# Filling the steps of a software pipeline: pieces cut to one step each, due at fixed steps or drawn by an account of TensorE time

## The chip, the core and the metric

The kernel runs on one core of a Trainium2 chip. The metric is the device time in microseconds of one execution. Three runs before the change took 5651.95, 5647.72 and 5645.32 us; the median is 5647.72 us. The profile is of one further execution.

The engines by the names of the profile: PE (TensorE, matrix products and transposes, with PEld for its weight loads), DVE (VectorE), ACT (ScalarE), POOL (GpSimd) and SP (SyncE, which issues nearly all transfers here). Each works through its own instructions in order and waits on semaphores for the others.

## What is computed

Four layers of attention follow each other on a state `x` of 2048 rows and 256 columns. All attend to the same 1601 context rows of 512 columns, and each adds its result to `x`. Layers 0, 2 and 3 have 16 heads of 64 and a column bias for a few token positions:

```python
q = hidden_states @ Wq;  k = encoder_hidden_states @ Wk;  v = encoder_hidden_states @ Wv
logits = einsum('bhqd,bhkd->bhqk', q, k) * HEAD_DIM ** (-0.5) + col_bias
probs = softmax(logits, axis=-1)
out = einsum('bhqk,bhkd->bhqd', probs, v) @ Wo + bo + residual
```

Layer 1 first divides each row of `x` by its root mean square. It has 16 query heads of 16 columns that share 4 heads of keys and values, and no bias. All is float32; in layer 1 the scores are formed from bfloat16 parts.

## The kernel before

**Units and steps.** A block is a pair of heads in layers 0, 2 and 3 (`Masked`, 8 blocks a layer) or one group of four query heads in layer 1 (`Grouped`, 4 blocks). A unit is one block on 512 of the 2048 queries, in `Grouped` one half of the block's heads on them: 4 units a block in `Masked`, 8 in `Grouped`, 32 a layer and 128 in all, numbered u0 to u127 here (layer 1 is u32 to u63). The 1601 keys are cut into 13 chunks, 12 of 128 and one of 65, and a unit passes through 13 steps, ca 0 to ca 12, one chunk a step. The loop at L1067 writes out 1664 such steps and a drain.

**What a step holds.** Three stages of neighbouring units overlap. In a step the loop emits the scores of a chunk of unit `ka`, the exponentials of a chunk of the unit before (15 steps later than its scores), and the product with the values (16 steps later). In a masked step this is on PE L751 (scores) and L869 (values); on ACT the copy of the scores to SBUF (L763) and the exponential (L841); on DVE the subtraction of the row maximum (L834) and the running maximum over chunks (L768); on POOL the running sum of the exponentials over chunks (L844 for chunks 0 and 1 together, then L846). A masked chunk is a tile `p` of 128 x 1024 in a pool of 17. At ca 0 and ca 1 PE also transposes the previous unit's maxima (L805) and spreads them (L818). In a grouped step PE does L784, L850, L855 and L869, DVE one reduction (L789) and ACT one exponential (L859). An instruction is held to the order written here on PE, ACT and DVE.

**Pieces.** What is left is cut into pieces, which the loop sprinkles over the steps, after the step's own work:

- for the next unit, `unit_groups`: load the transposed `x` (L735) and project the queries (L420 in masked units; L626, a split into parts, and stacks L529, L532, L645 in grouped ones);
- for a unit just finished, `finish_groups`: `denominators` (eight transposes of the sums, L888, reduced on DVE, L889, inverted, L890, and widened by POOL, L899), `divide` (four transposes, L907, and a product on DVE, L911) and two of `project` (L917, added to `xs` by DVE, L923);
- after the last block of a layer also `keep` or `normalize` (squares, `rms` with L679, and four `divide` of L689 and L691 for layer 1) or `rows_out`;
- for the next block, `key_groups`: the keys by 512 columns, one PE matmul of 512 columns a piece (L369, L559), and the values by two chunks (L384, L592), with their loads of the context (`context_slice`, L204).

PSUM holds two tiles `s`, one `b`, one `po` and one `pm`. All pieces work in the single `pm`, but for the transposes of the sums, which take one of the two `s` tiles that the scores use. A piece that wants `pm` waits until the engine that empties it, ACT or DVE, has done so.

**The order of the pieces.** `Pieces` (L970) keeps the queues `urgent`, `fill` and `later` and a credit. Unit pieces and finishing pieces enter `urgent` at ca 2; the next block's keys stand in `fill`, its values in `later` until ca 4 of the block's second unit. In every step but ca 0 and ca 1 after a masked unit, at least one piece is taken, `urgent` first, and more if what is left for the block is more than the steps. A key group of four pieces goes on over several steps.

## Time and profile before

| | us |
|---|---|
| median of three runs | 5647.72 |
| the profiled execution | 5653.54 |
| its span, first to last instruction | 5651.8 |
| from the start to the first step | 77.0 |
| u5 to u27 (steady masked units, layer 0) | 1003.8 |
| u28 to u35 (into layer 1) | 414.7 |
| u36 to u56 (steady grouped units) | 784.6 |
| u57 to u67 (out of layer 1) | 473.4 |
| u68 to u123 (steady masked units, layers 2 and 3) | 2459.1 |

A unit's time is the distance between the first score matmul of its first step and that of the next unit in the timeline of PE. A line of a group or of a timeline gives the source line, the engine, the operation, the tiles as out<-in, shapes, a count and the busy time; in square brackets or at the end stand the idle time before it and what ended that. In the view of waits a line names who waited for whom, with the total, the number and the longest wait in us. Matmul records overlap, so PE's work is better read from one start to the next than from durations.

### The profile page before, as it was taken

Reading aid. Unit: us, or ns where it says so; the run is one execution under the profiler, and the core shown is the slowest. Engines: PE = TensorE matmul, PEld = TensorE weight load, DVE = VectorE, ACT = ScalarE, POOL = GpSimd, SP = SyncE. Lnnn points to the kernel's source line nnn. Section 1 sums busy time; section 2 is a strip of 40 time slices with the busy share of each in tenths; the row PEclk is TensorE's granted clock in tenths of the full one; section 3 lists DMA queues with packets and bytes.
Section 4 is the critical chain, followed back from the end, with each engine's and each line's share of the span. In section 5 each row is a group of like instructions: output and inputs, shape, how many; then the busy total and the mean of one; then the engine's idle time right before and its main releaser. Section 6 shows DMA issues by size and latency. Waiting matters only on the chain.

```text
span 5651.8 us, 59516 instructions
## 1 busy us (share of the span) xinstructions
PE 5321.4 (94%) x22444; PEld 1865.2 (33%) x22444; DVE 4013.6 (71%) x4140; ACT 3196.2 (57%) x3513; POOL 2837.7 (50%) x1380
## 2 busy tenths in 40 slices
PE   6999999998889999999999999999999999999997
PEld 3333333332323333233233333333333333333332
DVE  3777777777765555555567777777777777777786
ACT  2666666665433434333456666666666666666665
POOL 1766666665410000000056666666666666666676
PEclk8999999999889999999999999999999999999998
DMA  4112211111100000001012111212111121111100
GB/s 135 32 57 60 59 49 53 55 56 44 39 20 5 9 9 9 9 13 52 15 51 61 56 54 49 57 56 59 46 56 55 54 59 49 53 56 52 54 17 15
DMA packets 209744, 252.88 MB, mean 45 GB/s; under 512 B 43529, under 2 KB 155401, under 8 KB 209456
## 3 DMA queue, kind: packets, MB, share of 16 engines
q1 hardware_dynamic: 206192, 243.69, 14.8%
q8 instruction: 177, 2.90, 0.2%
q0 software_dynamic: 1152, 3.28, 0.2%
q10 hardware_dynamic: 2112, 2.10, 0.1%
q14 instruction: 111, 0.91, 0.1%
HBM read 235.27 MB, written 13.76 MB: 44 GB/s over the span
## 4 chain that ended last, share of the span: by engine, by line
PE 78%; ACT 7%; POOL 7%; DVE 5%; issue 2%; DMA 0%; SPq 0%; ACTq 0%; POOLq 0%; DVEq 0%
PE po L869 24%; PE s L751 20%; PE pm L384 6%; PE pm L369 5%; PE pm L917 5%; POOL sums L844 4%; ACT p L763 4%; ACT p L841 3%; POOL sums L846 3%; PE s L850 2%; PE s L784 2%; PE pm L420 2%; PE s L805 2%; PE b L818 2%; PE s L855 2%
## 5 line engine op out<-in xcount | busy, mean ns | idle before, releaser
L846 POOL TENSOR_TENSOR sums<-sums,p 128x1024 f32<-128x1024 f32 (+1 forms) x1056 | 2499.2, 2367 | 1097.9 <-ACT p L841 1084.8
L763 ACT COPY p<-s 128x1024 f32<-128x1024 f32 (+1 forms) x1248 | 1263.4, 1012 | 1434.0 <-PE s L751 1138.3
L869 PE MATMUL po<-p,v 128*64 128x512 f32 (+1 forms) x6656 | 1821.7, 626 | 36.5 <-ACT p L841 34.7
L768 DVE TENSOR_TENSOR top<-s,top 128x1024 f32<-128x1024 f32 (+1 forms) x1056 | 1291.5, 1223 | 753.9 <-ACT p L763 749.4
L751 PE MATMUL s<-q,kT 64*128 64x512 f32 (+1 forms) x4992 | 1426.3, 648 | 117.6 <-DVE top L768 116.4
L834 DVE TENSOR_TENSOR p<-p,b 128x1024 f32<-128x1024 f32 (+1 forms) x1248 | 1504.7, 1206 | 2.4 <-PE b L818 2.0
L841 ACT ACTIVATE p<-p 128x1024 f32<-128x1024 f32 (+1 forms) x1248 | 1321.5, 1059 | 110.3 <-DVE p L834 109.4
L869 PEld LDWEIGHTS po<-p,v 128*64 128x64 f32 (+1 forms) x6656 | 332.0, 136 | 1032.1 <-issue 698.9
L899 POOL COPY by<-rden 128x512 f32<-128x512 f32 x128 | 78.5, 613 | 1111.8 <-DVE rden L897 1083.9
L751 PEld LDWEIGHTS s<-q,kT 64*128 64x128 f32 (+1 forms) x4992 | 370.7, 182 | 732.7 <-issue 454.6
L859 ACT ACTIVATE p<-s 128x1024 f32<-128x1024 f32 (+1 forms) x283 | 289.8, 1024 | 451.0 <-PE s L855 450.9
L844 POOL TENSOR_TENSOR sums<-p 128x1024 f32<-128x1024 f32 x96 | 226.5, 2360 | 434.2 <-ACT p L841 434.2
L789 DVE TENSOR_REDUCE row_top<-s 128x2 f32<-128x1024 f32 x261 | 318.6, 1221 | 122.9 <-PE s L784 121.9
L384 PEld LDWEIGHTS pm<-wv,ct 128*128 128x128 f32 (+1 forms) x2392 | 284.7, 187 | 218.9 <-issue 215.9
L384 PE MATMUL pm<-wv,ct 128*128 128x128 f32 (+1 forms) x2392 | 337.6, 286 | 0.5 <-ACT v L389 0.5
L369 PE MATMUL pm<-ct,wk 128*128 128x512 f32 (+1 forms) x736 | 315.8, 544 | 2.7 <-ACT kT L374 2.7
L917 PE MATMUL pm<-o,wo 128*128 128x512 f32 x512 | 292.0, 653 | 7.1 <-DVE xs L923 2.9
L859 ACT ACTIVATE p<-b 128x1024 f32<-128x1024 f32 (+1 forms) x133 | 136.2, 1024 | 217.8 <-PE b L855 217.8
L923 DVE TENSOR_TENSOR xs<-pm,xs 128x512 f32<-128x512 f32 x232 | 158.4, 683 | 90.4 <-PE pm L917 90.4
L806 DVE TENSOR_REDUCE ntop<-s 128x8 f32<-128x1024 f32 x96 | 117.6, 1225 | 130.9 <-PE s L805 130.6
L789 DVE TENSOR_REDUCE row_top<-b 128x2 f32<-128x1024 f32 x123 | 150.2, 1221 | 62.2 <-PE b L784 61.6
L420 PE MATMUL pm<-xT,wq 128*128 128x512 f32 x336 | 188.5, 644 | 0.0
(191 smaller groups left out, 3279.2 us busy)
## 6 DMA issues: line engine op xcount, KB each, us to landing
ct<-ctxT SPq DMA_DIRECT2D x288, 512.0 KB, 3.8
xT<-xT SPq DMA_DIRECT2D x104, 512.0 KB, 3.5
ct<-ctxT SPq DMA_DIRECT2D x48, 130.0 KB, 2.6
wk<-in_L_xattn_Wk_dram SPq DMA_DIRECT2D x24, 256.0 KB, 4.4
wv<-in_L_xattn_Wv_dram SPq DMA_DIRECT2D x24, 256.0 KB, 3.1
xT<-xs SPq DMA_DIRECT2D x12, 512.0 KB, 2.6
wq<-in_L_xattn_Wq_dram SPq DMA_DIRECT2D x24, 128.0 KB, 2.1
wo<-in_L_xattn_Wo_dram SPq DMA_DIRECT2D x24, 128.0 KB, 2.1
```

The costliest lines, as they stand in the source:

```text
L369: nc.tensor.matmul(u.pk[:, :n], u.wk[:, k, :], ct(k, a, n), start=(k == 0), stop=(k == NCT - 1),)
L384: nc.tensor.matmul(u.pv[:m, c - c0, :], ct(k, a, m), u.wv[:, k, :], start=(k == 0), stop=(k == NCT - 1),)
L751: nc.tensor.matmul(s[:m, h, :], self.u.kT[r, a : a + m], self.q[r, :], start=True, stop=(a != TAIL),)
L763: nc.scalar.copy(p[:m], s[:m])
L768: nc.vector.tensor_tensor(self.top[:m], s[:m], self.top[:m], ALU.max)
L789: nc.vector.tensor_reduce(self.top[:, :, q, k : k + 1], s, AX.X, ALU.max)
L834: nc.vector.tensor_tensor(self.p[c][:m], self.p[c][:m], self.less[:m], ALU.add)
L841: nc.scalar.activation(p[:m], p[:m], AF.Exp)
L844: nc.gpsimd.tensor_tensor(self.sums, self.p[0], p, ALU.add)
L846: nc.gpsimd.tensor_tensor(self.sums[:m], self.sums[:m], p[:m], ALU.add)
L869: nc.tensor.matmul(self.po[r, :], u.v[:m, c, r], self.p[c][:m, h, :], start=(c == 0), stop=(c == NT - 1),)
L917: nc.tensor.matmul(py, wo[:, ts(k, P)], self.o, start=True, stop=True)
```

## The change

- `Piece` is a function with a cost in units of about one key chunk. Every piece now starts and empties its PSUM tile itself. Keys are projected chunk by chunk (four matmuls of 128 columns, one copy), values chunk by chunk, queries in two halves of 256 columns. Before the first step, too, keys and values go chunk by chunk.
- `Pieces.at` puts a piece at a step of its own. Counted by ca of the unit in which they are emitted: the sums of the two heads at ca 3 and ca 4 (`denominators(0)`, `denominators(1)`), the query halves at ca 7 and 8, `divide` at ca 8, the projections at ca 10 and 11, the grouped stacks at ca 10, 11 and 12, normalisation from ca 12 on.
- The rest comes from `fill` when an account allows. In each step `share` is added (what is left, plus 7.0 a masked or 4.6 a grouped unit, over the steps left in the block), the cost of what is due is taken off, and a fill piece is taken while the credit is at least half its cost. The account is held between -1.5 and 1.5. `later` is released when the last unit of the previous block is finished.
- The denominators' transposes take `pm`, four at a time. The reciprocals no longer go through POOL, PE and DVE: SP writes them to DRAM, loads them back spread over the partitions, and POOL multiplies `oT` in place.
- The sums begin with a copy of chunk 0 on POOL, and chunk 1 is added as the others.
- The weights `wk` and `wv` have one buffer instead of two; a context tile holds two chunks; the loads of a block are issued three ahead, and `load_wo` at the block's third unit.

```diff
+Piece = namedtuple("Piece", "run cost")
...
-            u.wk = weights.tile([P, NCT, P], FP, name="wk")
-            u.wv = weights.tile([P, NCT, P], FP, name="wv")
+            u.wk = weights.tile([P, NCT, P], FP, name="wk", bufs=1)
+            u.wv = weights.tile([P, NCT, P], FP, name="wv", bufs=1)
...
+            def keys(c, ct):
...
+                pk = ps_m.tile([P, QB], FP, name="pm")[:, :m]
+                for k in range(NCT):
                     nc.tensor.matmul(
+                        pk, u.wk[:, k, :], ct(k)[:, :m], start=(k == 0), stop=(k == NCT - 1)
                     )
+                nc.scalar.copy(u.kT[:, a : a + m], pk)
...
+            return [(7 + j, Piece(lambda j=j: queries(j), 1.0)) for j in range(2)]
...
+            return found + [
+                (10, Piece(lambda: stacked(0), 0.5)), (11, Piece(lambda: stacked(1), 0.5)),
+                (12, Piece(last, 0.25)),
+            ]
...
+        return [
+            (10, Piece(squares, 0.0)), (11, Piece(rms, 2.0)),
+            *((12 + q, Piece(lambda q=q: divide(q), 0.0)) for q in range(QT)),
+        ]
...
+    def on_all_partitions(cols, to):
+        rows = dram.tile([2, P, QT], FP, name="cols", bufs=4)
+        with nc.allow_non_contiguous_dma(reason="1024 values, four at a time"):
+            nc.sync.dma_start(out=rows.rearrange("h p q -> p h q"), in_=cols)
+        for tile_, heads_ in to:
+            src = rows[heads_].rearrange("(o h) p q -> o (h p q)", o=1)
+            nc.sync.dma_start(out=tile_, in_=src.to_broadcast(tile_.shape))
...
-                if c == 1:
+                if c == 0:
                     self.sums = work.tile([P, 2, QB], FP, name="sums")
-                    nc.gpsimd.tensor_tensor(self.sums, self.p[0], p, ALU.add)
-                elif c:
+                    nc.gpsimd.tensor_copy(self.sums, p)
+                else:
                     nc.gpsimd.tensor_tensor(self.sums[:m], self.sums[:m], p[:m], ALU.add)
...
-        def denominators(self):
+        def denominators(self, h):
...
-                pt = ps_s.tile([P, 2, QT, P], FP, name="s")
...
+                pt = ps_m.tile([P, QT, P], FP, name="pm")
+                for q in range(QT):
+                    nc.tensor.transpose(pt[:, q, :], self.sums[:, h, ts(q, P)], ident)
+                nc.vector.tensor_reduce(rden[:, h, :], pt, AX.X, ALU.add)
+                if h == 0:
+                    return
                 nc.vector.reciprocal(rden, rden)
...
-            nc.gpsimd.tensor_copy(
-                self.by,
-                rden.rearrange("p h (q o) -> p q h o", o=1).to_broadcast((P, QT, 2, 64)),
-            )
+            by = work.tile([P, P, QT], FP, name="by", bufs=1)
+            on_all_partitions(
+                rden,
+                [(by[self.rows(h)].rearrange("r p q -> r (p q)"), slice(h, h + 1)) for h in range(2)],
+            )
+            self.by = by.rearrange("r p q -> r q p")
         def divide(self):
-            pr = ps_m.tile([P, QB], FP, name="pm")
...
-            nc.vector.tensor_tensor(self.o, pr, self.oT, ALU.mult)
+            oT = self.oT.rearrange("r (q p) -> r q p", p=P)
+            nc.gpsimd.tensor_tensor(oT, oT, self.by, ALU.mult)
...
+            found = [(1 + h, Piece(lambda h=h: self.denominators(h), 0.5)) for h in range(2)]
+            if not self.masked:
+                found = [(1, Piece(lambda: self.denominators(0), 1.0))]
+            found.append((6, Piece(self.divide, 0.0)))
+            return found + [(8 + k, Piece(lambda k=k: self.project(k), 1.0)) for k in range(NC)]
...
+        def step(self, step, share, cost):
+
+            self.credit = max(min(self.credit + share - cost, 1.5), -1.5)
+            for piece in self.due.pop(step, ()):
+                piece.run()
+                self.credit -= piece.cost
+            while self.fill and self.credit >= self.fill[0].cost / 2:
+                piece = self.fill.popleft()
+                piece.run()
+                self.credit -= piece.cost
...
+        if scoring and ca == 5 and ka + 1 < len(units):
             ahead = unit_of(ka + 1)
+            pieces.at(step - ca, ahead.layer.query_pieces(ahead))
         if valuing and cv == NT - 1:
+            pieces.at(step, valuing.finish() + after(kv))
+
+            if units[kv + 1 : kv + 2] and units[kv + 1][0] != units[kv][0]:
+                pieces.release()
+        share = 0.0
+        if scoring:
+            units_left = NB * len(scoring.layer.SUBS) - place - ca / NT
+            own = 7.0 if scoring.masked else 4.6
+            share = (pieces.left() + own * units_left) / (NT * units_left)
+        pieces.step(step, share, 1.0 if top and top.masked else 0.0)
```

## The prediction

> **What bounds the kernel now.** I read the page's busy shares first, then the waits, then PE's timeline step by step.

> ```profile
> PE 5321.4 (94%) x22444; PEld 1865.2 (33%) x22444; DVE 4013.6 (71%) x4140; ACT 3196.2 (57%) x3513; POOL 2837.7 (50%) x1380
> ```

> PE is the bound, and nearly everywhere. So only PE work, and waits that end on PE, move the time. These are the waits that the change aims at:

> ```profile
> ACT p L763 <- POOL sums L844: 174.5, 93, 2.5
> PE s L751 <- DVE top L768: 116.4, 71, 2.7
> PE pm L907 <- POOL by L899: 55.9, 79, 4.4
> ```

> One chain: at ca 3 POOL adds chunks 0 and 1 together and so frees chunk 0's tile too late for the score copy of ca 4. The copy is late, the maximum after it too, and L888 holds the other `s` tile. The scores of ca 5 wait 1.71. The next rows, from the timeline, show what the change brings instead: two pieces of one step that both want `pm`, with DVE to empty it.

> ```profile
> 2942.62 1.13 PE L751 MATMUL s<-q,kT 64*128 64x512 f32 x4
> 2944.69 1.12 PE L917 MATMUL pm<-o,wo 128*128 128x512 f32 x2
> 2945.38 1.22 DVE L768 TENSOR_TENSOR top<-s,top 128x1024 f32<-128x1024 f32 x1
> 2946.51 0.68 DVE L923 TENSOR_TENSOR xs<-pm,xs 128x512 f32<-128x512 f32 x1
> 2947.24 1.12 PE L917 MATMUL pm<-o,wo 128*128 128x512 f32 x2 [1.43 <-DVE xs L923]
> 2948.30 1.13 PE L751 MATMUL s<-q,kT 64*128 64x512 f32 x4
> ```

> DVE empties `pm` only after this step's running maximum, which waits for the score copy. `pm` is free 4.62 after the step's start; the step takes 5.68, where one piece gives 3.12.

> **Steady masked blocks (u5 to u27, u68 to u123, about 20 blocks).** Prices are starts to starts in u18: scores 1.06, values 1.01, so 2.07 a step; L805 or L818 1.02; a value chunk 1.09; a query matmul or projection 1.05; eight transposes 0.97, L907's four 0.59. A key chunk has the value chunk's form, eight instructions of 128 columns, so 1.09, against 1.06 for the old 512-column piece. The tail chunk is taken at 0.65, the bias at 0.15 a unit.

> Before, a unit has 13 x 2.07 + 2.04 + 0.15 + 2 x 1.05 + 0.97 + 0.59 + 2 x 1.05 = 34.9, a block four of these plus 12 x 1.06 + 0.65 + 13 x 1.09 = 27.5, so 167.0. Measured are (1050.5 for u4 to u27 + 2459.1) / 20 = 175.5: waits are 8.5 a block. After, the denominators are two times four transposes (2 x 0.59) and L907 is gone: 34.5 a unit; the fill is 25 x 1.09 + 0.65 = 27.9; together 165.9.

> Then I carried the account through by hand. A block repeats: units with 7, 6, 7 and 6 fill pieces. A fill piece falls into ca 3 or ca 4 beside a denominator five times a block (ca 3; ca 4; ca 3 and ca 4; ca 4), beside a projection at ca 10 once, and two keys share ca 12 once. Beside a denominator: PE is ready at 2.07 + 0.59 = 2.66; DVE's maximum of the step ends at 3.5 (scores 1.06, copy from 1.23, maximum from 2.28, in the steps about 2914), the reduction of 512 columns is 0.70 (as L791's of 520), so `pm` is free at about 4.25. In the rows above it is 4.62 (DVE was late there by a `divide` that is gone), in u29, projection then L559, 4.35. The wait is 1.6 (0.8 if the reduction ran ahead of the maximum, 2.0 by 4.62). Beside the projection it is 1.1 (u29 shows 1.16), between two keys, emptied by ACT, 0.45. A block: 5 x 1.6 + 1.1 + 0.45 = 9.6. Steps with less than one piece cost 0.4, where DVE's 1.21 + 1.22 outlast PE's 2.07. Half-clock windows are left at 0.5. So 165.9 + 10.5 = 176.4, +0.9 a block, **+18 in all**. The waits shown go, all 8.5 of them but the clock; `pm` is late next, for 9.6. Ends: -80 with 0.8, +55 with 2.0.

> What lies beside: POOL's copy of chunk 0 is 1.2 (twice L899's 0.61) and the multiply 1.2 (half of L846's 2.37), in 41 to 44 a unit where POOL has 28 to 31; chunk 0's tile is then free by 4.6 of ca 2 and asked for at ca 4. ACT gains about 0.6 a unit for shorter copies, with 28 of 43 busy. DVE loses L911's 0.69 and gains little.

> **The way over DRAM.** SP's queue gets a write of 256 pieces of 16 bytes, which waits for the reciprocal, then two loads, which wait for the write; behind them stand the next unit's `x` (ca 5) and the context loads. The reciprocal is done at 4.3 of ca 4. The nearest rows are the token indices (1 KB, 3.2 to land) and `wo` (16 KB, 1.7). Multiply at ca 8, 12 later: hidden. The `x` load is issued after about 4.3 + 0.4 + 2.4 + 0.9 = 8.0 and lands 3.5 later, at 11.5; the first query half wants it at ca 7, 11.05 after ca 4's start where ca 4 holds no fill (one unit a block), later elsewhere. 0.45 x 20 gives 9, halved for masked layers' first blocks and luck: **+5**, between 0 and, with 3.2 to land, 25. Context loads run three tiles, six chunks, ahead, and the single `wk` and `wv` are refilled two steps before their first reader: hidden, but for the start.

> [...]

> **Start, +15.** Before the first step keys and values come in 26 pieces, each emptied by ACT before the next (L384 of one chunk 1.09 with 0.3 to 0.46 idle): about 11.8 for each slice of four chunks against 9.4 now (53.1 to 62.5), +7. The first key of the next block waits for `wk`: 3 more. `later` is released only when an earlier block's last unit is finished, and block 0 has none: its values are flushed at u4, ca 0, 13 x 1.55 = 20 at once, while u1 to u3 run short steps (36 to 37 where u3 has 39.6 with waits): +5. Ends +5, +25.

> **Into layer 1 (u28 to u35), -35.** Now 414.7, with half-clock stretches. By the prices: u28 is 34.5 + 7 key chunks 7.6 + two waits 3.2 = 45; u29 is 34.5 + chunks 6.1 + four stacks 2.0 + six pairs about 6.3 = 49; u30 is 34.5 + stacks 1.6 + six chunks of 64 columns at 0.67 = 4.0 + waits 4.5 = 45. In u31 to u34 `rms` stands at ca 0 and a `divide` in each of ca 1 to ca 4, and those steps are DVE's: a `divide` is 0.94 + 2 x 0.61 to 1.97, and such steps last 4.62 and 5.13 in u30 now. At 5.2 they give 26 for ca 0 to ca 4 of u31, and 29 for its eight others: 55; u32 likewise 26 + 25 = 51; u33 and u34, where the masked DVE work ends, 48 and 42; u35 38 as now. That is 373; for pairs not counted I take 380. Gone are the groups of 512 keys with their splits and the waits of L907; kept is DVE. Ends -65, 0.

> **Grouped units, +15.** A unit without queries is 35.8. L907 leaves (-0.48) and the wait for a split at once used leaves (-0.3); but projection and stack now share ca 10 and ca 11, and PE waits for DVE's 0.69, 0.9 from end to end (L917 to L923 at 1815): +1.8. Net 0.9 a pair, +10 for u36 to u56; u57 to u63, with fill, +5. Ends 0, +30. **u64 to u67, -7**: the same prices with 185.5 for 192.7; 0 to -12. **End, 0**: u124 to u126 lose the chain (-7), the drain gains the way over DRAM and POOL's copy and multiply (+7); -5 to +8.

> **Sum.** 18 + 5 + 15 - 35 + 15 - 7 + 0 = +11. The profiled execution took 5653.5, 0.1% over the median; against it the sum is 5665, on the median's scale 5647.7 + 11 = 5659, written as 5660. A change under 0.2% (11 us) cannot be told here.

> **Rivals.** *The waits for `pm` are short, and it is faster.* Emptying happens at 3.5 of the step, 0.8 a pair: 100 pairs give 80 less, 5580. For it: the transposes are ready at 2.66. Against: DVE is held to the written order, the maximum comes first. It decides below 1.45 a pair.

> *SP's queue makes `x` late, and it is much slower.* If the write takes 5.0 to land instead of 2.4, `x` lands at 14.1 of ca 4; the query half waits 3.0 in the unit with a bare ca 4, and 0.4 in the three others, where ca 4 takes 5.35 and the half is wanted at 13.7: 24 x 3.0 + 72 x 0.4 = 101, so 5755. For it: the write is 256 pieces of 16 bytes, and no row has such a form. Against: rows of that many bytes end at 3.2. It decides from 4.7 on, where three units in four begin to wait.

> *The clock halves, and it is slower.* At 484.6 to 488.0 PE idled 1.72, and the clock stood at 0.51 in the next 3.4. The step lost 0.9 (4.25 for 3.34). If 100 waits of 1.6 did that, +90: 5750. Against: 1.43 idle at 2850 left the clock at 1.00. [...] The trace shows a halving after 1.72, and the measurement decides.

> *No change within 0.2%*: the same mechanism with a better layer change, 5645.

> **Chances.** The forecast, its own range 5625 to 5700: 0.52. Short waits: 0.26. SP late: 0.10. Clock: 0.09. Something unnamed: 0.03. Faster by over 0.2% (below 5636): 0.26 and a tenth from the forecast's lower side, 0.36. Same: 0.16. Slower: 0.48. The range goes from 5575, the short waits with their 80, to 5730, near the slow rivals: 2 in 10 lie outside.

> **What would show it.** In steady masked units: no wait of ACT for the first POOL sum; PE waits for DVE's reduction of the denominators (`rden`), five a block, 1.6 each; steps of 5.3 at ca 3 and ca 4; units of about 44, 42.5, 46 and 43. In grouped units, PE waits for `xs` before stacks, 0.9. A lump of some 20 at u4. u28 to u35 at 380. Wrong it is if those waits are absent or half, if `x` or `by` is waited for on PE or POOL, or if the half-clock share grows.

## The result and the profile after

The changed kernel takes 5704.6 us, the median of four runs (5703.7 to 5715.2), beside 5649.7 (5645.3 to 5652.0) for the kernel before. The ratio is 1.0103, with a 95% interval of 1.0090 to 1.0115: 1% slower. The profiled execution took 5715.2 us, its span 5713.5; it is the slowest of the four, 0.2% over the median. The times by stage below come from it and are compared with the profiled execution before, whose span was 5651.8; so they add up to 61.7, where the medians differ by 54.9.

| stage | before, us | after, us | measured | predicted |
|---|---|---|---|---|
| to the first step, and u0 to u4 | 295.8 | 306.7 | +10.8 | +15 |
| u5 to u27 and u68 to u123, steady masked | 3462.9 | 3482.3 | +19.4 | +18, and +5 for a late `x` |
| u28 to u35, into layer 1 | 414.7 | 412.6 | -2.0 | -35 |
| u36 to u63, grouped | 1065.3 | 1109.4 | +44.1 | +15 |
| u64 to u67 | 192.7 | 188.2 | -4.4 | -7 |
| u124 to the end | 220.5 | 214.3 | -6.2 | 0 |
| sum | 5651.8 | 5713.5 | +61.7 | +11 |

Line numbers are from here on those of the kernel that ran: in the changed kernel L370 is a key chunk, L381 a value chunk, L889 the transposes of the sums and L890 their reduction to `rden`, L512 the first matmul of a stack, L921 the addition that empties a projection, and L909 POOL's multiplication of `oT`. First the page's busy times after, then four lines of its waits (who waited for whom: total us, times, longest):

```profile
PE 5292.8 (93%) x24180; PEld 2075.3 (36%) x24180; DVE 3971.8 (70%) x4183; ACT 3259.2 (57%) x4000; POOL 3053.0 (53%) x1476
```

```profile
PE pm L381 <- DVE rden L890: 88.6, 59, 1.6
...
PE pm L370 <- DVE rden L890: 63.1, 41, 1.6
...
PE pm L512 <- DVE xs L921: 48.2, 59, 2.8
...
PE s L751 <- DVE top L768: 2.8, 2, 2.4
```

PE is busy 28.6 less than before, though 1736 instructions more pass through it, and the span is 61.7 longer. So the time went into waits. The old chain is gone: the scores wait 2.8 for DVE's maximum, where it was 116.4. In its place PE waits 100 times for `rden`, the reduction of the denominators (88.6 + 63.1 = 151.7), and 59 times for `xs`, a projection that is emptied ahead of a stack. One of the 100, step ca 3 of u84, in the timeline:

```profile
3743.24 1.13 PE L751 MATMUL s<-q,kT 64*128 64x512 f32 x4
...
3744.47 1.01 ACT L763 COPY p<-s 128x1024 f32<-128x1024 f32 x1 [0.55 <-PE s L751]
...
3745.31 0.66 PE L889 MATMUL pm<-ident,sums 128*128 128x128 f32 x4
...
3745.51 1.23 DVE L768 TENSOR_TENSOR top<-s,top 128x1024 f32<-128x1024 f32 x1 [0.81 <-ACT p L763]
...
3746.65 0.68 DVE L890 TENSOR_REDUCE rden<-pm 128x4 f32<-128x512 f32 x1
...
3747.39 1.16 PE L370 MATMUL pm<-ct,wk 128*128 128x128 f32 x8 [1.43 <-DVE rden L890]
3748.48 1.13 PE L751 MATMUL s<-q,kT 64*128 64x512 f32 x4
```

PE has issued the four transposes 0.6 after 3745.31. DVE does not reduce them until its running maximum has ended, and that waits for ACT's copy of the scores. The key chunk, which is the next to want `pm`, stands 1.43, and the step takes 5.24. The steady units typically take 44.0, 42.7, 46.3 and 42.7.

### The profile page after: what moved, and what is told of

The parts are those of the page before. It is cut to its first block, busy times and chain, and to the rows that moved or that the text cites. A ratio compares the mean times of both kernels' runs of the same rounds, so it can differ in the third digit from the quotient of the medians.

```text
span 5713.5 us, 64559 instructions
## 1 busy us (share of the span) xinstructions
PE 5292.8 (93%) x24180; PEld 2075.3 (36%) x24180; DVE 3971.8 (70%) x4183; ACT 3259.2 (57%) x4000; POOL 3053.0 (53%) x1476
## 3 DMA queue, kind: packets, MB, share of 16 engines
q14 instruction: 123, 1.01, 0.1%
## 4 chain that ended last, share of the span: by engine, by line
PE 79%; DVE 10%; ACT 5%; issue 3%; POOL 1%; DMA 1%; SPq 0%; ACTq 0%; POOLq 0%; DVEq 0%
PE po L869 24%; PE s L751 20%; PE pm L381 6%; PE pm L370 6%; PE pm L915 4%; PE pm L405 3%; ACT p L763 3%; DVE top L768 3%; PE s L850 2%; PE s L784 2%; DVE p L834 2%; PE s L805 2%; PE b L818 2%; PE s L855 2%; DVE rden L890 1%
## 5 line engine op out<-in xcount | busy, mean ns | idle before, releaser
L846 POOL TENSOR_TENSOR sums<-sums,p 128x1024 f32<-128x1024 f32 (+1 forms) x1152 | 2724.8, 2365 | 1212.3 <-ACT p L841 1182.2
L763 ACT COPY p<-s 128x1024 f32<-128x1024 f32 (+1 forms) x1248 | 1262.4, 1012 | 1111.0 <-PE s L751 960.1
L768 DVE TENSOR_TENSOR top<-s,top 128x1024 f32<-128x1024 f32 (+1 forms) x1056 | 1292.1, 1224 | 847.5 <-ACT p L763 845.7
L834 DVE TENSOR_TENSOR p<-p,b 128x1024 f32<-128x1024 f32 (+1 forms) x1248 | 1505.6, 1207 | 2.6 <-PE b L818 1.9
L751 PE MATMUL s<-q,kT 64*128 64x512 f32 (+1 forms) x4992 | 1418.2, 645 | 4.1 <-DVE top L768 2.8
L909 POOL TENSOR_TENSOR oT<-oT,by 128x512 f32<-128x512 f32 x128 | 198.6, 1551 | 1118.9 <-DMA by<-cols 710.9
L751 PEld LDWEIGHTS s<-q,kT 64*128 64x128 f32 (+1 forms) x4992 | 367.4, 181 | 416.5 <-issue 229.5
L381 PE MATMUL pm<-wv,ct 128*128 128x128 f32 (+1 forms) x2392 | 345.3, 287 | 114.8 <-DVE rden L890 88.6
L789 DVE TENSOR_REDUCE row_top<-s 128x2 f32<-128x1024 f32 x261 | 318.9, 1223 | 165.9 <-PE s L784 164.6
L370 PE MATMUL pm<-ct,wk 128*128 128x128 f32 (+1 forms) x2392 | 346.2, 288 | 74.3 <-DVE rden L890 63.1
L381 PEld LDWEIGHTS pm<-wv,ct 128*128 128x128 f32 (+1 forms) x2392 | 287.4, 187 | 317.2 <-issue 122.5
L370 PEld LDWEIGHTS pm<-ct,wk 128*128 128x128 f32 x2392 | 290.5, 192 | 281.9 <-issue 125.5
L915 PE MATMUL pm<-oT,wo 128*128 128x512 f32 x512 | 291.9, 652 | 13.3 <-POOL oT L909 12.5
L921 DVE TENSOR_TENSOR xs<-pm,xs 128x512 f32<-128x512 f32 x232 | 158.6, 684 | 98.4 <-PE pm L915 98.4
L384 ACT COPY v<-pm 128x128 f32<-128x128 f32 (+1 forms) x312 | 83.1, 266 | 220.8 <-PE pm L381 212.6
```

The lines of the kernel that those rows point to most:

```text
L370: nc.tensor.matmul(pk, u.wk[:, k, :], ct(k)[:, :m], start=(k == 0), stop=(k == NCT - 1))
L381: nc.tensor.matmul(pv, ct(k)[:, :m], u.wv[:, k, :], start=(k == 0), stop=(k == NCT - 1))
L751: nc.tensor.matmul(s[:m, h, :], self.u.kT[r, a : a + m], self.q[r, :], start=True, stop=(a != TAIL),)
L763: nc.scalar.copy(p[:m], s[:m])
L768: nc.vector.tensor_tensor(self.top[:m], s[:m], self.top[:m], ALU.max)
L789: nc.vector.tensor_reduce(self.top[:, :, q, k : k + 1], s, AX.X, ALU.max)
```

## The experiments

The theory has three parts. In the masked units the loss is the emptying of `pm` by DVE, where a fill piece follows a denominator. In the grouped units it is the same, between a projection and a stack. On the way into layer 1 it is DVE, which is held up by something that the prediction had not priced. The rivals stand with each experiment. An experiment with one run (e3 to e7 and e10) is read by the stages of its profile, not by its total. How far a stage moves by itself is seen where the edit does not touch it: u5 to u27 and u68 to u123 together took 3468.3 to 3482.3 in the five profiles of kernels that are alike there (the changed kernel, e3, e4, e6 and e7), and u28 to u31 took 234.8 in the changed kernel and 232.9 in e6.

### Fill first (e1)

```diff
-            for piece in self.due.pop(step, ()):
-                piece.run()
-                self.credit -= piece.cost
+            due = self.due.pop(step, ())
+            self.credit -= sum(piece.cost for piece in due)
             while self.fill and self.credit >= self.fill[0].cost / 2:
...
+            for piece in due:
+                piece.run()
```

> The changed kernel with one thing swapped: in every step the fill piece runs ahead of the pieces that are due, at the same steps as before. Theory (a pair of pieces costs what the emptying of the first one costs; DVE empties a denominator only after the running maximum of the step, ACT empties a key or value chunk at once): the wait of 1.52 beside a denominator becomes one on ACT's copy, 0.4 as between two keys at ca 12 (0.36), and the one beside the projection 0.4 instead of 1.08. 5 x 1.1 + 0.7 = 6.2 a block, 20 blocks, 125 less: 5580 (5560 to 5610), steps with a denominator and a fill piece 4.1 to 4.3 instead of 5.24 and 5.45. Rival (those steps are bound by DVE's or ACT's own work, the order in pm does not matter): the steps stay above 5, 5695 to 5710.

Measured: 5579.0 us (5575.1 to 5583.2), ratio to the kernel before 0.9890 (0.9873 to 0.9906). u68 to u123 take 2385.4 instead of 2467.8. The same step of u84:

```profile
3664.57 1.13 PE L751 MATMUL s<-q,kT 64*128 64x512 f32 x4
...
3666.63 1.16 PE L370 MATMUL pm<-ct,wk 128*128 128x128 f32 x8
...
3667.83 0.27 ACT L373 COPY kT<-pm 128x128 f32<-128x128 f32 x1
...
3668.24 0.63 PE L889 MATMUL pm<-ident,sums 128*128 128x128 f32 x4 [0.45 <-ACT kT L373]
3668.80 0.70 PE L751 MATMUL s<-q,kT 64*128 64x512 f32 x2
```

The same pieces stand in the same step, in the other order. The wait is 0.45, the step 4.23. DVE's reduction falls into the next step; in the whole kernel no matmul of a key or value chunk (L370, L381) waits for it any more. So the length of the wait belongs to the engine that empties the first tile, and not to the work in the step.

### A copy for chunk 0, alone, in the kernel before (e2)

```diff
-                if c == 1:
+                if c == 0:
                     self.sums = work.tile([P, 2, QB], FP, name="sums")
-                    nc.gpsimd.tensor_tensor(self.sums, self.p[0], p, ALU.add)
-                elif c:
+                    nc.gpsimd.tensor_copy(self.sums, p)
+                else:
```

> The kernel before with one part of the change alone: POOL begins the sums with a copy of chunk 0 and adds chunk 1 as the others. Theory (the chain at ca 3 to ca 5 begins with the double add that frees chunk 0 too late): the 174.5 us in which ACT waits for the first sum go, and with them the 116.4 in which the scores wait for DVE; 5530 (5510 to 5560). Rival (the other s tile is still held by the transposes of the sums, so the scores of ca 5 wait for that instead): 5630 to 5655, and the wait of the scores for DVE stays at 80 or more.

Measured: 5537.0 us (5529.2 to 5537.7), ratio 0.9808 (0.9792 to 0.9825). The waits of this kernel:

```profile
ACT p L763 <- POOL sums L844: 58.6, 86, 1.0
...
PE s L751 <- DVE top L768: 29.8, 71, 1.9
```

The chain begins where the prediction put it, and one edit of POOL's cuts it: 174.5 falls to 58.6 and 116.4 to 29.8. The theory said that the waits vanish; they shrink, those of the scores from 1.64 to 0.42 each. Part of the gain is clock: in u68 to u123 the granted clock was halved for 44 us before and for 7 here. This part of the change alone makes the kernel 1.9% faster. In the changed kernel the new pairs ate it.

### POOL's additions left out on the way into layer 1 (e3)

```diff
                 if c == 0:
                     self.sums = work.tile([P, 2, QB], FP, name="sums")
-                    nc.gpsimd.tensor_copy(self.sums, p)
-                else:
+                    if self.l == 0 and u.n == self.layer.BLOCKS - 1:
+                        nc.gpsimd.memset(self.sums, 1.0)
+                    else:
+                        nc.gpsimd.tensor_copy(self.sums, p)
+                elif self.l or u.n < self.layer.BLOCKS - 1:
```

> The changed kernel without POOL's additions in the last block of layer 0 (u28 to u31): the sums of these units are a constant, their output is not the reference's. Theory (DVE operations that read and write SBUF alone are held until POOL's running instruction ends: 8 of 13 casts of the split took 1.07 to 2.29 instead of 0.22 and ended 0.04 to 0.08 after the end of a POOL addition; what is held delays the subtraction, the exponential and PE): all casts take 0.2 to 0.4, and u28 to u31 take 212 to 222 instead of 234.8. Rival (the casts are short where nothing is held, but PE waits for the number of DVE's pieces and for pm, not for the holds): u28 to u31 stay at 231 to 236.

What led to it are these lines of the changed kernel at u28 ca 6 and ca 7, first DVE's timeline, then POOL's:

```profile
1346.91 0.29 DVE L503 SCALAR_TENSOR_TENSOR rest<-pm,ka 64x128 f32<-64x128 f32 x1 [0.23 <-ACT ka L500]
1347.24 1.72 DVE L506 CAST ka<-rest 64x128 bf16<-64x128 f32 x1
1349.00 1.51 DVE L507 TENSOR_TENSOR kb<-rest,ka 64x128 bf16<-64x128 f32 x1
1350.54 1.22 DVE L834 TENSOR_TENSOR p<-p,b 128x1024 f32<-128x1024 f32 x1
```

```profile
1346.52 2.35 POOL L846 TENSOR_TENSOR sums<-sums,p 128x1024 f32<-128x1024 f32 x1 [4.07 <-ACT p L841]
1348.83 1.52 POOL L909 TENSOR_TENSOR oT<-oT,by 128x512 f32<-128x512 f32 x1
```

The cast of 64 x 128 ends at 1348.96, 0.09 after POOL's addition; the difference behind it ends at 1350.51, 0.16 after POOL's multiply. Where POOL is idle the same two take 0.22 and 0.29. The subtraction, which releases the exponential and then PE, starts 2.7 late. Of the 13 casts, nine began when a POOL instruction had 0.15 or more to run; their median is 1.95, and all nine ended 0.06 to 0.18 after POOL's instruction did. The other four took 0.22.

Measured: u28 to u31 take 220.8 instead of 234.8, u32 to u35 172.5 instead of 177.9. The line of the normalisation's products, L678, over all its instructions (duration in ns, min/median/max), in the changed kernel and then here:

```profile
L678 DVE SCALAR_TENSOR_TENSOR xT<-xs,normw,rest x32: 339/350/2509, 1497.2 to 1671.3; 128x128 f32<-128x128 f32 x32
```

```profile
L678 DVE SCALAR_TENSOR_TENSOR xT<-xs,normw,rest x32: 344/348/353, 1476.9 to 1638.2; 128x128 f32<-128x128 f32 x32
```

In the changed kernel five of the 32 began while a POOL addition had 1.5 or more to run; they took 1.69 to 2.43. A sixth began 0.02 before an addition and took 2.51; one that began 0.09 before one took 0.35. Of three others that began under a POOL instruction, two found only 0.16 of it left and took 0.35, and one ran beside a fill with zeros (a memset, which only writes), with 1.35 of it left, and took 0.34. Here no addition runs beside them, and none takes over 0.36. The casts of u28 are still held here, since the exponentials of u27 run then, with their additions. From u29 ca 2 on, where those of u28 begin, all take 0.22 but one: that one takes 0.81 and begins while POOL multiplies (L909's place). The hold is shown by taking POOL's work away. The stretch gets 19.4 shorter by it. A part of that is clock: it stood at half for 68 us of the eight units in the changed kernel and for 58 here, so up to 5 of the 19.4. Tiles that come free earlier are no rival: ACT's waits for POOL's sums were 2.7 in the eight units of the changed kernel and are 1.5 here.

So the cast L506, the difference L507 and the products L678, which all read and write SBUF alone, were held: L506 took up to 2.29 instead of 0.22, L507 once 1.51 instead of 0.29, L678 up to 2.51 instead of 0.35. Not held were L678 beside the memset (0.34) and, beside POOL's additions, L503, L834 and L890, which take one input out of PSUM (the longest L503 of 64 x 128 took 0.30, the longest L834 1.22, the longest L890 0.69). The theory's 'read and write SBUF alone' is wider than what the trace shows: the reciprocal L893 does that too, it began 91 times while an addition of POOL had 1.5 or more to run, and it never took over 0.21. The order of the starts does not decide it alone either, as the two L678 that began 0.02 and 0.09 ahead of an addition show.

### The split finished for 512 columns at once (e4)

```diff
-                self.split(pk, self.ka[:, a : a + m], self.kb[:, a : a + m], 1.0)
+                nc.scalar.copy(self.ka[:, a : a + m], pk)
...
+                nc.vector.tensor_tensor(
+                    self.rest[top, d : d + m], pk[top], self.ka[top, a : a + m], ALU.subtract
+                )
+                if c % 4 == 3 or c == NT - 1:
...
+                    nc.vector.tensor_copy(self.ka[top, whole], less)
+                    nc.vector.tensor_tensor(
+                        self.kb[top, whole], less, self.ka[top, whole], ALU.subtract
+                    )
```

> The changed kernel with the split of layer 1's keys finished once for 512 columns: per chunk still ACT's copy and DVE's difference out of PSUM, which frees pm, but the cast and the second difference once in four chunks (4 instead of 13 each). Theory (held casts): 9 of 13 holds of 1.5 go; u28 to u31 take 221 to 228 instead of 234.8. Rival (the number of pieces that want pm makes the excess, or DVE's own time, of which only 9 x 0.5 = 4.5 goes, beside other work): 231 to 236.

Measured: u28 to u31 take 226.2, so 8.6 less, of which u28 has 6.4. All four casts that are left are held (1.19 to 2.09). The 8.6 are more than the 4.5 of the work of the nine that went, as the theory said, but the clock stood at half for 34 us instead of 44, which can be up to 5 of them. So it is not shown here that the holds, and not the work, made the gain.

### A denominator counted as a whole piece (e5)

```diff
-            found = [(1 + h, Piece(lambda h=h: self.denominators(h), 0.5)) for h in range(2)]
+            found = [(1 + h, Piece(lambda h=h: self.denominators(h), 1.0)) for h in range(2)]
...
-            own = 7.0 if scoring.masked else 4.6
+            own = 8.0 if scoring.masked else 4.6
```

> The changed kernel with the account alone altered: a denominator counts as a whole piece (1.0 instead of 0.5), a masked unit's own work as 8.0 instead of 7.0. The order within a step is as in the changed kernel. By the account, in u68 to u123 1 fill piece instead of 70 then stands beside a denominator, 14 beside a projection as before, 32 steps hold two fill pieces (15 before), 13 a fill piece and a query half, 28 fill pieces a step of the maxima (1 before). Theory (the wait belongs to the tile that DVE empties, not to the number of pieces in a step): a block waits 1.1 beside the projection and some 0.4 at 3.2 pairs that ACT empties, 2.4 instead of 9.6; u68 to u123 take 2360 to 2395 instead of 2467.8, the whole 5570 to 5600. Rival (a unit has too many pieces for its 13 steps, and any pair costs about 1.5): 4.3 pairs a block instead of 6 to 7, u68 to u123 2430 to 2460.

Measured: 5572.3 us, u68 to u123 2368.4. The group lines of value chunks and key chunks in the changed kernel (busy us, mean ns | idle before them and what ended it), then in this one:

```profile
L370 PE MATMUL pm<-ct,wk 128*128 128x128 f32 (+1 forms) x2392 | 346.2, 288 | 74.3 <-DVE rden L890 63.1 <-ACT kT L373 9.4 <-DMA wk<-in_L_xattn_Wk_dram 1.3
L381 PE MATMUL pm<-wv,ct 128*128 128x128 f32 (+1 forms) x2392 | 345.3, 287 | 114.8 <-DVE rden L890 88.6 <-DVE xs L921 18.4 <-ACT v L384 5.8
```

```profile
L370 PE MATMUL pm<-ct,wk 128*128 128x128 f32 (+1 forms) x2392 | 344.5, 287 | 33.7 <-DVE xs L921 16.3 <-ACT q L408 8.1 <-ACT kT L373 5.3
L381 PE MATMUL pm<-wv,ct 128*128 128x128 f32 (+1 forms) x2392 | 344.4, 287 | 39.1 <-ACT v L384 30.8 <-DVE rden L890 4.5 <-DVE xs L921 1.9
```

The pieces and their work are the same to 2 us. The idle time of the two falls from 189.1 to 72.8; of what is left ACT ends the most, and `rden` 4.5 instead of 151.7. There are still steps with two pieces; they are pairs that cost little.

### Layer 1's projections away from the stacks (e6)

```diff
-            return found + [(8 + k, Piece(lambda k=k: self.project(k), 1.0)) for k in range(NC)]
+            at = 8 if self.masked else 11
+            return found + [(at + k, Piece(lambda k=k: self.project(k), 1.0)) for k in range(NC)]
...
-            return [(10, Piece(lambda: keep(l + 1, b), 0.0))]
+            return [(13, Piece(lambda: keep(l + 1, b), 0.0))]
```

> The changed kernel with layer 1's projections at ca 0 and ca 1 of the next unit instead of ca 10 and ca 11, where the stacks stand (the store of the finished rows, too, three steps later). Theory (in every unit of layer 1, not in every second, PE waits twice for DVE to empty the projection ahead of the stack: 4.84 a step, of which 2.30 + 0.95 + 0.64 is work, so 0.95 is wait): 1.9 a unit goes, u36 to u56 take 775 to 785 instead of 818.4, u57 to u63 277 to 283 instead of 291.0; the steps with stacks last 2.94. Rival (the stacks wait for the parts of the queries or for DVE's queue anyway, and at ca 0 and ca 1 the maxima's chain on DVE takes the projection's emptying in): 800 to 820.

Measured: u36 to u56 take 770.4, u57 to u63 278.6, the whole 5644.0. The group line of the stacks' first matmul, in the changed kernel and then here:

```profile
L512 PE MATMUL pm<-q,sel_qa 128*128 128x512 bf16 x64 | 24.3, 379 | 51.3 <-DVE xs L921 45.4 <-DVE xs L919 5.9
```

```profile
L512 PE MATMUL pm<-q,sel_qa 128*128 128x512 bf16 x64 | 25.1, 392 | 5.6 <-DVE xs L919 5.6
```

The stack steps take 2.94 (u48 ca 10 and ca 11) instead of 4.83 and 4.84. The gain, 48.0 for 21 units or 2.3 a unit, is more than the 1.9 of the pair; it probably helps that the projection at ca 1 now also covers a wait at ca 2 for DVE's `max_rows` (1.04 in u48 of the changed kernel, 0.18 here).

### The divides earlier (e7)

```diff
-            (10, Piece(squares, 0.0)), (11, Piece(rms, 2.0)),
-            *((12 + q, Piece(lambda q=q: divide(q), 0.0)) for q in range(QT)),
+            (9, Piece(squares, 0.0)), (10, Piece(rms, 2.0)),
+            *((11 + min(q, 2), Piece(lambda q=q: divide(q), 0.0)) for q in range(QT)),
```

> The changed kernel with the normalisation one step earlier and its four divides at ca 0, ca 1, ca 2 and ca 2 instead of ca 1 to ca 4. Theory (at ca 3 and ca 4 of u31 and u32 the divide stands ahead of the denominator's reduction in DVE's queue, and PE waits for the reduction with the next piece for pm: 8.06 in one step of u31, 3.97 in one of u32): u31 and u32 together lose 8 to 14 of 118. Rival (DVE has the same work and the same holds, only elsewhere, and PE waits for the exponentials at ca 0 to ca 2 instead): u31 and u32 within 3 of 118.

Measured: u31 and u32 take 65.5 + 46.7 = 112.2 instead of 118.0, 5.8 less: between the two. The lump at u31 ca 4 shrank from 12.82 to 6.40, but ca 3 of the same unit grew from 3.68 to 5.87, and in u32 PE still waits 3.62 at ca 3, for ACT behind a held divide. u29, which the edit does not touch, also moved, by 4.4: it had 10.2 us at half clock in the changed kernel and 0.3 here. So one run cannot tell these 5.8 well. The whole took 5706.4, no less than the changed kernel. The step in which the divide and the reduction collide got shorter, and a part of its work only moved to the steps beside it.

### Together (e8 and e9)

```diff
-            if units[kv + 1 : kv + 2] and units[kv + 1][0] != units[kv][0]:
+            if kv == 0 or units[kv + 1 : kv + 2] and units[kv + 1][0] != units[kv][0]:
                 pieces.release()
```

This edit releases the first block's values at its second unit; with it come fill first, the split for 512 columns, the late projections and the early divides.

> The changed kernel with fill pieces first in a step, the late projections of layer 1, the early divides, the split finished for 512 columns at once, and the first block's values released at the second unit instead of all at u4. If the terms are independent: 5579 - 51 (grouped) - 8 (split) - 8 (divides) - 0 to 5 (first block): 5505 to 5515. If they overlap in u28 to u35, where fill first alone already took 13: 5515 to 5530. If the late projections give their gain back: 5555 to 5575.

Measured: 5507.2 us (5504.9 to 5512.3), ratio 0.9743 (0.9726 to 0.9759). The total lies where the independent terms had put it, but not term by term. Beside e1, u36 to u63 give 64 (51 had been set; u36 to u56 take 767.6), u28 to u35 give 11 (16 had been set; u28 to u31 take 220.6, 225.2 in e1), u0 to u4 give 7 (0 to 5 had been allowed), and the part before the first step takes 9 more, 86.9 for 78.0, on another chip.

Next, the account with whole pieces in addition (the diff of that section):

> The kernel with all these edits (fill first, late projections, early divides, split for 512 columns, first block's values at the second unit), and in addition the account that counts a denominator as a whole piece and a masked unit's own work as 8.0. Theory (the two cures of the masked wait do not add up: fill first made the waits short, the account takes the pairs away, so only the better of the two counts): steady masked units as with the account alone (972.0 and 2368.4 for u5 to u27 and u68 to u123, against 980.9 and 2389.5), the rest as together: 5475 to 5490. Rival (they add up, because the pairs that are left wait for ACT alone): another 1 to 2 a block, 5445 to 5470.

Measured: 5456.5 us (5454.5 to 5458.4), ratio 0.9651 (0.9635 to 0.9667), 4.3% less than the changed kernel's 5704.6. The theory that only the better cure counts falls, though the other adds little. u5 to u27 take 967.7, u68 to u123 2357.3, which is 0.8 a block less than with the account alone, where the rival had 1 to 2. A block lasts 42.3 + 41.4 + 42.5 + 42.1 = 168.3, of which 165.9 is work by the prediction's prices. The rest of the difference comes from elsewhere: beside e8, 7.2 came from u28 to u31 (213.4) and 4.0 from u0 to u4.

### The reciprocals over PE again (e10)

```diff
-            on_all_partitions(
-                rden,
...
+            nc.gpsimd.tensor_copy(
+                self.by,
+                rden.rearrange("p h (q o) -> p q h o", o=1).to_broadcast((P, QT, 2, 64)),
+            )
...
-            nc.gpsimd.tensor_tensor(oT, oT, self.by, ALU.mult)
+            pr = ps_m.tile([P, QB], FP, name="pm")
...
+            nc.vector.tensor_tensor(self.oT, pr, self.oT, ALU.mult)
...
-            found.append((6, Piece(self.divide, 0.0)))
+            found.append((4, Piece(self.divide, 0.0)))
```

> The last kernel with the reciprocals taken the old way: POOL widens them, PE transposes them (four transposes), DVE multiplies out of pm, at ca 6. It prices the way over DRAM by itself. Theory (the way over DRAM is hidden: the write lands in 2.2, the loads in 3.2, PE never waited for the product; PE's work is time): 96 x 0.59 + 32 x 0.48 = 72 comes back, and where a fill piece stands at ca 6 some 0.4 of wait for ACT, at most 38: 72 to 110 more than the kernel beside it. Rival (POOL's wait for the loads and its multiply of 1.55 delay the sums and so the chunks' tiles, and that is paid somewhere): under 50 more, or a gain.

Measured: 5558.7 us, 102.2 more than the kernel with the way over DRAM. The group line of the four transposes:

```profile
L924 PE MATMUL pm<-ident,by 128*128 128x128 f32 x512 | 81.7, 282 | 45.9 <-ACT v L384 21.0 <-ACT kT L373 19.2 <-DVE rest L541 2.3
```

By the prediction's prices 72 is work; 45.9 is waiting for `pm`, which has one more piece to hold. Together that is 16 more than the 102.2; 8.5 of it is the drain, the rest stays open. Only the drain gains (96.0 instead of 104.5): there PE waits for the product of the way over DRAM, twice, 12.4 in all. Everywhere else PE never waits for it, and the change made something good there.

## Why the prediction was right or wrong

The side was right, the size not: 5704.6 against 5660, or +55 for +11, inside the range, above the forecast's own 5625 to 5700. That it still lies inside is in part luck: the upper end, 5730, was set for the two slow rivals, and neither came; what took the time up there were two terms that were 33 and 29 short.

- **Steady masked blocks, right.** 176.3 a block (2467.8 / 14) against 176.4. The account carried through by hand gave the pieces of every step: 70 of the waits for `rden` stand in the 14 blocks of u68 to u123, five a block. The wait came out at 151.7 / 100 = 1.52 against 1.6. The rival of short waits needed less than 1.45. The order of DVE's queue, with the maximum first, decides it, as e1 and e5 show from two sides. The old waits went, as said: 116.4 fell to 2.8, and the 174.5 of ACT for the first sum to 1.6. It took more than the copy of chunk 0, with which alone 29.8 and 58.6 stay. The low end of this term, '-80 with 0.8', is the difference to the forecast and not the sum, which would be 18 - 80 = -62.
- **`x` late, nothing.** The write takes 2.2 to land (median of 128, at most 3.4), not 5.0, and none of the 672 query matmuls out of `xT` waited at all. The term of +5 was too careful, and the rival that rested on it falls. POOL's multiply was mis-sized, 1.55 instead of 1.2. POOL did wait for `by`, which the prediction had named as a sign of being wrong: 36 times, 710.9 in all, but nearly all of it in layer 1, where POOL has little else to do. PE waits for the product only in the drain, twice, 12.5.
- **The clock, right to leave it small.** In u68 to u123 it was halved for 17 us, where it was 44 before; in u5 to u27 for 17, where it was 14. In all these units it was halved after 10 of the 97 waits for `rden`, at 1.6 us each (the rival had 0.9): 16, where 0.5 a block had been allowed, 10 in all.
- **Start, right:** +10.8 for +15. The part before the first step took 77 to 87 with the same code on different chips, so it is compared on one: 71.1 in e2, whose start is the old one, and 78.0 in e1, which has the new one. That is +7, as predicted.
- **Into layer 1, wrong: -2.0 for -35.** The step that failed is the pricing of u28 to u31 by PE's work and `pm` pairs: 45 + 49 + 45 + 55, where 54.6, 60.6, 51.3 and 68.3 were measured. It named 'the groups of 512 keys with their splits' as gone, but the splits are not gone: 13 replace 4, and a cast of 0.22 costs up to 2.29 under a POOL addition. The prediction had read the products of a divide as lasting '2 x 0.61 to 1.97' (a row of 0.61 holds both of them, so '2 x' is too much) and did not ask what made the difference. Removing the additions gave back 14.0 + 5.4 of the missing 33, up to 5 of it by the clock; fewer casts gave 8.6 of the same, and the divides up to 5.8. The clock is another part: it stood at half for 44 of the 234.8 us, so at most 22 were lost to it, some of them a result of these waits. It was not priced. With all edits of e9 the four units take 213.4, still 19 above the 194 predicted; how that divides into clock, holds of the casts of u28 and divides stays open.
- **Grouped units, wrong by its size: +44.1 for +15.** The mechanism was right: the pair costs 1.9 in a unit (two steps of 4.84, of which 3.89 is work). The failed step is 'Net 0.9 a pair, +10 for u36 to u56': it sets the waits against L907 as if they came once in two units. They come in every unit, so 1.9 - 0.48 = 1.4, times 21 is 30; 33.9 was measured, and 10.3 instead of 5 in u57 to u63. The term's own ends, 0 and +30, do not hold the +44.1. The 0.3 for the split's wait did not come either: PE waits at ca 2 for `max_rows`, with or without a stack behind it (1.04 in u48 in both kernels).
- **End, -6.2 for 0:** u124 to u126 lost 6.1, near the 7 said; the drain, which should have gained 7, stayed (103.3 to 103.1). Its longest wait before, 10.5 of PE for POOL's sums, fell to 1.9, and PE waits 3.8 and 8.7 for the product of the way over DRAM instead.

## What to carry to other kernels

When pieces share one buffer, the price of two in a step is set by the engine that empties the first, and by what stands ahead of it in that engine's queue; put the piece with the quick emptying first, or let the account count the slow one as a full step. Count a wait by how often its step occurs (per unit, per pair, per block), and check that count before the multiplication. Before small DVE instructions with SBUF operands are made more numerous, look at what POOL runs beside them: here nine casts of 13 lasted until POOL's addition or copy had ended, a median of 1.95 instead of 0.22.

## What the runs showed of the hardware that was not expected

**A DVE instruction held by POOL.** In the changed kernel the nine casts of the split that began while a POOL instruction had 0.15 us or more to run took a median of 1.95, the other four 0.22; six of the 32 L678 were held and took 1.69 to 2.51, the others 0.34 to 0.35. The instructions with an input from PSUM were not held (L503 of 64 x 128 took at most 0.30, L834 1.22, L890 0.69), nor was the reciprocal L893 (at most 0.21), and POOL's memset did not hold L678 (0.34).

**A halved clock after 1.6 us, if the wait begins at the right moment.** In the steady masked units of the changed kernel PE waited 1.43 in 55 steps at ca 3 and ca 4, and the clock was never halved after one; it waited about 1.63 in 42 steps of ca 4, and after 10 of these it was halved for 3.4 us. One of the ten, at u119, in the timeline of PE, and the same stretch in windows (the last three columns are granted clock, DMA share and GB/s):

```profile
5293.32 0.66 PE L889 MATMUL pm<-ident,sums 128*128 128x128 f32 x4
5295.61 1.16 PE L381 MATMUL pm<-wv,ct 128*128 128x128 f32 x8 [1.64 <-DVE rden L890]
5296.70 1.59 PE L751 MATMUL s<-q,kT 64*128 64x512 f32 x4
5298.21 1.98 PE L869 MATMUL po<-p,v 128*64 128x512 f32 x4
```

```profile
5293.00:5297.00 4.00, 2.36 (x16) 1.69 (x16) 3.84 (x5) 1.75 (x3) 3.25 (x2) 1.00 0.04 1
5297.00:5300.60 3.60, 3.60 (x10) 0.78 (x7) 1.18 (x2) 2.04 (x3) 0.51 (x2) 0.53 0.22 52
```

A unit with such a halving lasts 1.6 longer (u105 and u109 44.28, u97 and u113 42.68). How many waits fall so differs from run to run: the five profiles that are alike in u5 to u27 and u68 to u123 have 1, 4, 6, 8 and 10 halvings there and take 3468.3, 3472.5, 3476.2, 3479.2 and 3482.3. Less 1.6 for each halving, all five come to 3466.1 to 3466.7. So the spread of these stages is the phase of the waits. In e1 and e5, where no such wait is left in these units, not one halving occurs in u5 to u27 and u68 to u123.
